# Local attention: where the softmax weights are divided by their sums, and which way round the values are multiplied

## The chip, the cores and the metric

The kernel runs on one core of a Trainium2 chip. A core has five engines, each with its own queue of instructions that it works off in the order written: PE (TensorE, matrix products into PSUM), DVE (VectorE), ACT (ScalarE), POOL (GpSimd) and SP (SyncE, which here issues transfers). They run side by side and wait for one another through semaphores. The metric is the time of one execution on the device in microseconds; lower is better.

## The reference

The program is one forward pass through four stages, each added to its input: six layers of an attention with a distance term, a mixture of experts, a state-space block, and a local transformer of two layers. Only the last stage is touched. Its attention works on B = 8 sequences of 256 tokens, with 8 heads of 64 features. Cut to what matters:

```python
q = l2norm(q) * qs;  k = l2norm(k) * ksc
q, k = rotary_xpos(q, k)
# windows of 64 queries; each sees its own 64 keys and the 64 before
sim  = einsum('bhwid,bhwjd->bhwij', bq * 8, bk)
sim  = where(mask, -max, sim)                 # i < j or i > j + 64 or j == -1
attn = softmax(sim, axis=-1)
out  = einsum('bhwij,bhwjd->bhwid', attn, bv)
x    = x + out_as_rows @ wo                   # then a gated feed-forward
```

The softmax may be divided by its sum before or after the product with the values. The result is the same up to rounding.

## The kernel before, in words

Local attention is `attention(l, b, t0)`: one block is one layer l (2) and one sequence b (8), 16 blocks in all. A block handles its 256 tokens as two chunks c of 128 queries. Chunk 0 takes keys 0 to 127. Chunk 1 is two windows of 64 queries: queries 128 to 191 with keys 64 to 191, and queries 192 to 255 with keys 128 to 255. So values are needed from three starting points: `("v", 0)`, `("v", 1)` and `("v", 2)` begin at token 0, 64 and 128. `P` is 128 and `HF` is 64.

The steps of a block are these, with the lines of the kernel before.

- `project` (1284): queries, keys or values from the tokens, one 128x512 bank of PSUM each. There are 7 projections: two chunks of keys and of queries, three of values. `value` (1290) copies the values to SBUF on ACT.
- `square` and `norms` (1295, 1315): squares on ACT and their sums over a head on DVE. `inverse` (1320 to 1322) makes the inverse norms: a maximum on DVE, then a logarithm and an exponential on ACT.
- `rotate` (1303 to 1307): three multiplies on DVE into r1 and r2 (three buffers each); `add` (1326) on POOL sums them; `unit_keys` (1330) on POOL scales the keys, a 128x512 tile by a column for each head.
- `turn` and `turned` (1338, 1344): transposes on PE, and the copy to SBUF on ACT.
- `scores` (1351, 1360): the mask is added by a matmul with the identity, then the products; `top` (1371, 1374): the negated maximum of each row on DVE.
- `expo(c, par)` (1383): exponentials on ACT of four of the eight heads (par 0 the even ones, par 1 the odd ones); each also leaves its row sum in `rz`.
- `turn_e` and `turned_e` (1392, 1399, 1401): the exponentials are transposed, four heads at a time; the copy is DVE's for even heads, ACT's for odd ones.
- `values` (1409): the turned exponentials are the weights of the matmul, the values stream through; the output has tokens on the partitions.
- `divide` (1416, 1418): reciprocal of the sums and a multiply on DVE, from PSUM into o.
- `turn_o` and `turned_o` (1426, 1432): o is transposed, so that features are on the partitions, and copied to `ot` on ACT.
- `out_proj` (1437) and `residual` (1443): the product with wo, and the addition to the tokens on DVE.

Around these stand `enter` (1256 to 1271), which normalises and turns the next sequence in the first layer, and `feed_forward` (1471 to 1540), once for each two sequences: turn_in, stats, scale (its `rs`, lines 81 and 82 on POOL), norm (hk, line 1242), products pg and pa (1500), gelu (1506, with loads of an activation table on both sides), pff (1520), and a residual `y<-pff` (1532).

The order of the work is written out by hand. Every step is put down with `at(slot, order, fn)`. A block begins 16 slots after the one before it, so up to three pieces of different blocks are interleaved. The slots are then worked through in order, inside a slot by the number `order`, and with equal numbers by who was put down first. What a step issues goes to the end of the queue of each engine it uses. No scheduler changes this order. PSUM has 8 banks here: 3 for scores, and 5 that all other products share; a product waits until one of these is free.

```python
(13, 4, turn_e, 0, 0), (13, 4, turn_e, 0, 1), (14, 4, turned_e, 0, 0), (14, 2, turned_e, 0, 1),
(15, 4, values, 0, 0), (15, 4, values, 0, 1), (17, 2, divide, 0), (18, 2, turn_o, 0), (19, 3, turned_o, 0),
```

Of the kernel before, what the change touches and what calls it, by code (L numbers as in the profile page):

```python
# [10 lines left out]
F32 = mybir.dt.float32  # L11
# [3 lines left out]
ALU = mybir.AluOpType  # L15
# [3 lines left out]
P = 128  # L19
# [16 lines left out]
DEPTH1, HEADS1, DH1, WIN = 2, 8, 64, 64  # L36
# [19 lines left out]
def model_kernel(ctx: ExitStack, tc: tile.TileContext, A: dict, out: bass.AP):  # L56
    nc = tc.nc
# [3 lines left out]
    small = ctx.enter_context(tc.tile_pool(name="small", bufs=4))  # L61
# [10 lines left out]
    ident = const.tile([P, P], F32, name="ident", tag="ident")  # L72
# [108 lines left out]
    with ExitStack() as s0:  # L181
# [3 lines left out]
        wk = s0.enter_context(tc.tile_pool(name="wk", bufs=2))  # L185
# [4 lines left out]
        ps_m = s0.enter_context(tc.tile_pool(name="ps_m", bufs=2, space=PSUM))  # L190
# [11 lines left out]
        for b in range(NB):  # L202
            h = hp.tile([P, NC, P], F32, name="h", tag=f"h{b}")
# [24 lines left out]
        def at(slot, order, fn):  # L228
            slots.setdefault(slot, []).append((order, len(slots[slot]) if slot in slots else 0, fn))
# [645 lines left out]
    with ExitStack() as s2:  # L875
        c2 = s2.enter_context(tc.tile_pool(name="c2", bufs=1))
        wk = s2.enter_context(tc.tile_pool(name="swk", bufs=2))
# [3 lines left out]
        ps_m = s2.enter_context(tc.tile_pool(name="ps_mm", bufs=1, space=PSUM))  # L881
# [301 lines left out]
    with ExitStack() as s3:  # L1183
        c3 = s3.enter_context(tc.tile_pool(name="c3", bufs=1))
        wk = s3.enter_context(tc.tile_pool(name="lwk", bufs=2))
        ps_s = s3.enter_context(tc.tile_pool(name="ps_sl", bufs=3, space=PSUM))
        ps_m = s3.enter_context(tc.tile_pool(name="ps_ml", bufs=5, space=PSUM))
# [6 lines left out]
        HF = P // 2  # L1194
# [81 lines left out]
        def attention(l, b, t0):  # L1276
            v = {}
# [8 lines left out]
                v["p", key] = pq  # L1286

            def value(key):
                vt = wk.tile([P, INNER], F32, name="v", tag=f"v{key}")
                nc.scalar.copy(vt, v["p", key])  # L1290
                v["v", key] = vt

            def square(c, i):
# [83 lines left out]
            def expo(c, par):  # L1377
                if par == 0:
                    v["e", c] = wk.tile([P, 2, 4, P], F32, name="el", tag="el")
                    v["rz", c] = small.tile([P, HEADS1], F32, name="rz", tag="rz", bufs=3)  # L1380
                for j in range(4):
                    h = 2 * j + par
                    nc.scalar.activation(  # L1383
                        v["e", c][:, par, j, :], v["s", c][par][:, j, :], AF.Exp,
                        scale=v["rn", c][:, 0, h : h + 1], bias=v["nm", c][:, par, j : j + 1],
                        accum_out=v["rz", c][:, h : h + 1],
                    )

            def turn_e(c, par):
                pt = ps_m.tile([P, 4, P], F32, name="pte", tag="m")  # L1390
                for j in range(4):
                    nc.tensor.transpose(pt[:, j, :], v["e", c][:, par, j, :], ident)  # L1392
                v["pe", c, par] = pt
# [6 lines left out]
                else:  # L1400
                    nc.scalar.copy(v["et", c][:, par], v["pe", c, par])

            def values(c, half):
                if half == 0:
                    v["pav", c] = ps_m.tile([P, HEADS1, DH1], F32, name="pav", tag="m")
                for h in range(4 * half, 4 * half + 4):
                    hd = h * DH1
                    for q0, nq, key in [(0, P, 0)] if c == 0 else [(0, HF, 1), (HF, HF, 2)]:
                        nc.tensor.matmul(  # L1409
                            v["pav", c][q0 : q0 + nq, h, :], v["et", c][:, h % 2, h // 2, q0 : q0 + nq],  # L1410
                            v["v", key][:, hd : hd + DH1], start=True, stop=True,
                        )

            def divide(c):
                rz = v["rz", c]
                nc.vector.reciprocal(rz, rz)
                o = wk.tile([P, HEADS1, DH1], F32, name="o", tag="o")
                nc.vector.tensor_tensor(  # L1418
                    o, v["pav", c], rz.unsqueeze(2).to_broadcast([P, HEADS1, DH1]), ALU.mult
                )  # L1420
                v["o", c] = o.rearrange("p h d -> p (h d)")

            def turn_o(c):
                pt = ps_m.tile([P, 4, P], F32, name="pto", tag="m")
                for k in range(4):
                    nc.tensor.transpose(pt[:, k, :], v["o", c][:, k * P : (k + 1) * P], ident)
                v["po", c] = pt

            def turned_o(c):
                if c == 0:  # L1430
                    v["ot"] = wk.tile([P, 4, T], F32, name="ot", tag="ot")
                nc.scalar.copy(v["ot"][:, :, c * P : (c + 1) * P], v["po", c])

            def out_proj():
                pn = ps_m.tile([P, T], F32, name="pn", tag="m")
# [9 lines left out]
            for slot, order, fn, *args in (  # L1445
                (0, 3, project, (0, 1), 1, 0), (1, 4, square, 0, 1), (1, 4, rotate, 0, 1), (2, 5, norms, 0, 1), (2, 6, add, 0, 1),
                (1, 3, project, (0, 0), 0, 0), (2, 4, square, 0, 0), (2, 4, rotate, 0, 0), (3, 5, norms, 0, 0), (3, 6, add, 0, 0),
                (4, 5, inverse, 0), (5, 6, unit_keys, 0),
                (2, 3, project, 0, 2, 0), (3, 4, value, 0),
                (3, 3, project, (1, 1), 1, P), (4, 4, square, 1, 1), (4, 4, rotate, 1, 1), (5, 5, norms, 1, 1), (5, 5, add, 1, 1),  # L1450
                (4, 3, project, (1, 0), 0, P), (5, 4, square, 1, 0), (5, 4, rotate, 1, 0), (6, 5, norms, 1, 0), (6, 6, add, 1, 0),
                (7, 5, inverse, 1), (8, 6, unit_keys, 1),
                (5, 3, project, 1, 2, HF), (6, 4, value, 1),
                (6, 3, project, 2, 2, P), (7, 4, value, 2),
                (5, 5, turn, 0, 0), (6, 5, turned, 0, 0), (7, 5, turn, 0, 1), (8, 3, turned, 0, 1),
                (8, 5, turn, 1, 0), (9, 4, turned, 1, 0), (10, 4, turn, 1, 1), (11, 4, turned, 1, 1),
                (9, 3, scores, 0), (10, 2, top, 0), (11, 3, expo, 0, 0), (12, 3, expo, 0, 1),
                (12, 3, scores, 1), (13, 2, top, 1), (14, 3, expo, 1, 0), (15, 3, expo, 1, 1),
                (13, 4, turn_e, 0, 0), (13, 4, turn_e, 0, 1), (14, 4, turned_e, 0, 0), (14, 2, turned_e, 0, 1),
                (15, 4, values, 0, 0), (15, 4, values, 0, 1), (17, 2, divide, 0), (18, 2, turn_o, 0), (19, 3, turned_o, 0),  # L1460
                (16, 4, turn_e, 1, 0), (16, 4, turn_e, 1, 1), (17, 3, turned_e, 1, 0), (17, 3, turned_e, 1, 1),
                (18, 4, values, 1, 0), (19, 4, values, 1, 1), (20, 2, divide, 1), (21, 2, turn_o, 1), (22, 3, turned_o, 1),
                (23, 4, out_proj), (24, 3, residual),
            ):
                at(t0 + slot, order, lambda fn=fn, args=args: fn(*args))

# [84 lines left out]
        for n in range(DEPTH1 * NB):  # L1551
            l, b = n // NB, n % NB
            if l == 0:
                enter(b, SLOTS * n)
            attention(l, b, SLOTS * n)
            if b % 2 == 1:
                feed_forward(l, b - 1, SLOTS * n)
# [96 lines left out]
```

## Time and profile before

| what | value |
|---|---|
| three runs | 2004.97, 2005.86, 2011.44 us; median 2005.86 us |
| profiled execution | 2002.59 us, its span 2000.8 us |
| mean granted clock of PE | 0.944 |
| PE busy | 1702.5 us (85%) |
| DVE busy | 1441.5 us (72%) |
| ACT busy | 1285.3 us (64%) |
| POOL busy | 1107.4 us (55%) |
| local transformer, first to last | about 1520 us to 2000.8 us of the span |

Durations in what follows are of the profiled execution. A busy PE is not PE at its peak, as matmuls overlap and their ends are modelled. A line number is one of the kernel before, if not said otherwise. In an answer in order of time the columns are start, length, engine and line; a bracket says how long the engine stood idle before it and what released it.

### The profile page before, as it was taken

To read this page: it belongs to the slowest core of one execution; us is meant where nothing else is said; L and a number is where in the kernel's file an instruction comes from. 1 tells how busy PE (TensorE), PEld (TensorE's weight loads), DVE (VectorE), ACT (ScalarE), POOL (GpSimd) and SP (SyncE) were. 2 spreads that over 40 slices of the span, in tenths; PEclk is the share of its full clock that TensorE was granted. 3 is DMA by queue.
4 is the path that set the end of the run, shared out by engine and by line. 5 is a ranking of instruction groups with operands and counts; after the bars stand their busy time and mean duration, and the time that the engine had idled before them with its cause. 6 is when DMAs were issued, how large, how long until landed. Compare 5 with 4: busy or idle time off the path is not lost. (4 is left out here: it accounts for less than half of the span.)

```text
span 2000.8 us, 38671 instructions
## 1 busy us (share of the span) xinstructions
PE 1702.5 (85%) x13390; PEld 999.1 (50%) x13406; DVE 1441.5 (72%) x3339; ACT 1285.3 (64%) x4570; POOL 1107.4 (55%) x1641
## 2 busy tenths in 40 slices
PE   5899999999999999998768867687666898888987
PEld 2565655655655655655444542222122555555554
DVE  4778787878787878786655436988897777666664
ACT  4787888888888888886541324443532666666664
POOL 2477777777777777777763024767564332233221
PEclk9999999999999999998888979888878999999999
DMA  9200000000000000000000310000000000000000
GB/s 306 70 2 2 21 4 2 15 11 1 8 17 2 2 24 2 2 2 4 7 5 7 111 38 2 4 6 0 1 0 1 1 1 1 1 1 1 6 6 11
DMA packets 43218, 35.52 MB, mean 18 GB/s; under 512 B 3957, under 2 KB 39055, under 8 KB 43023
## 3 DMA queue, kind: packets, MB, share of 16 engines
q1 hardware_dynamic: 41423, 30.63, 5.0%
q8 instruction: 108, 1.77, 0.4%
q0 software_dynamic: 1024, 2.10, 0.4%
q14 instruction: 87, 0.71, 0.1%
q10 hardware_dynamic: 576, 0.31, 0.1%
HBM read 20.57 MB, written 12.45 MB: 17 GB/s over the span
## 5 line engine op out<-in xcount | busy, mean ns | idle before, releaser
L334 ACT ACTIVATE e<-s,nmax 128x256 f32<-128x256 f32 x1536 | 708.9, 490 | 96.2 <-DVE nmax L330 93.2
L330 DVE TENSOR_REDUCE nmax<-s 128x2 f32<-128x512 f32 x768 | 493.9, 671 | 147.0 <-PE s L320 146.9
L334 ACT ACTIVATION_READ_ACCUMULATOR e<-s,nmax 128x1 f32 x1536 | 341.4, 222 | 0.0
L320 PE MATMUL s<-kt,qm 32*128 32x256 f32 x3072 | 304.9, 423 | 18.4 <-ACT e L334 15.8
L371 PE MATMUL pacc<-e,dg 128*32 128x256 f32 x3072 | 257.5, 396 | 41.7 <-POOL dg L344 28.5
L320 PEld LDWEIGHTS s<-kt,qm 32*128 32x128 f32 x3072 | 184.5, 191 | 116.2 <-ACT e L334 65.9
L1104 POOL TENSOR_TENSOR hc<-h,bc 128x1024 f32<-128x1024 f32 x64 | 155.4, 2433 | 114.3 <-DVE h L1097 106.1
L1326 POOL TENSOR_TENSOR r<-r,r 128x512 f32<-128x512 f32 x64 | 81.1, 1271 | 225.5 <-DVE r L1307 179.5
L344 POOL TENSOR_TENSOR dg<-sel,z 128x256 f32<-128x256 f32 x192 | 118.4, 617 | 132.2 <-DVE z L342 113.4
L1086 ACT ACTIVATE da<-pd,na 128x510 f32<-128x510 f32 x128 | 80.8, 682 | 166.2 <-PE pd L1069 154.5
L371 PEld LDWEIGHTS pacc<-e,dg 128*32 128x32 f32 x3072 | 95.8, 111 | 166.1 <-POOL dg L344 61.1
L1097 DVE TENSOR_TENSOR_SCAN h<-da,pu 128x1024 f32<-128x1024 f32 x64 | 146.4, 2287 | 8.5 <-DVE pu L1095 0.5
L81 POOL TENSOR_SCALAR rs<-mv 128x2 f32<-128x2 f32 (+1 forms) x192 | 44.3, 230 | 190.3 <-DVE mv L237 103.4
L82 POOL TENSOR_TENSOR rs<-rs,mhalf 128x2 f32<-128x2 f32 (+1 forms) x192 | 140.4, 732 | 15.7
L1383 ACT ACTIVATE el<-sl,nm,rn 128x128 f32<-128x128 f32 x256 | 114.0, 466 | 37.7 <-DVE nm L1374 37.5
L1069 PE MATMUL pu<-u,ssel 32*128 32x512 f32 x256 | 95.0, 749 | 49.8 <-DVE h L1097 39.9
L1283 PE MATMUL pq<-wqkv,y 128*128 128x512 f32 x224 | 119.7, 620 | 1.0 <-DVE y L1271 1.0
L381 ACT ACTIVATE nw<-pacc 128x256 f32<-128x256 f32 x96 | 36.9, 384 | 118.6 <-PE pacc L367 117.6
L459 PE MATMUL pf<-h2t,wa 128*128 128x256 f32 x384 | 106.9, 402 | 0.0
L475 PE MATMUL po<-wf,r 128*128 128x128 f32 x768 | 101.9, 288 | 2.4 <-DVE r L469 2.4
L475 PEld LDWEIGHTS po<-wf,r 128*128 128x128 f32 x768 | 93.6, 198 | 16.9 <-DVE st L235 13.6
L302 POOL TENSOR_TENSOR qm<-qt,kmask 128x1024 f32<-128x1024 f32 x48 | 90.9, 1895 | 0.4 <-DVE qt L291 0.4
(302 smaller groups left out, 3480.9 us busy)
## 6 DMA issues: line engine op xcount, KB each, us to landing
bucket<-zrow SPq DMA_DIRECT2D x1, 8640.0 KB
ln<-in_ln_dram SPq DMA_DIRECT2D x6, 448.0 KB, 3.7
wa<-in_wa_dram SPq DMA_DIRECT2D x6, 384.0 KB, 3.1
wf<-in_wf_dram SPq DMA_DIRECT2D x6, 256.0 KB, 2.7
wqkv<-in_wqkv_dram SPq DMA_DIRECT2D x1, 1536.0 KB, 6.2
xb<-bucket SPq DMA_DIRECT2D x23, 64.0 KB, 1.9
routed<-ob SPq DMA_DIRECT2D x23, 64.0 KB, 1.6
w<-in_w1e_dram SPq DMA_DIRECT2D x1, 1408.0 KB, 33.4
```

What stands on the lines that cost most here:

```text
L82: nc.gpsimd.tensor_tensor(dst, dst, mhalf.to_broadcast(list(dst.shape)), ALU.pow)
L320: nc.tensor.matmul(ss[g][:, i, :], v["qm"][rows, 2 * k + i].rearrange("p j q -> p (j q)"), v["kt"][rows, :], start=True, stop=True,)
L330: nc.vector.tensor_reduce(v["nmax", k][:, g, :], v["s", k][g], AX.X, ALU.max, negate=True)
L334: nc.scalar.activation(v["e", k][:, g, i, :], v["s", k][g][:, i, :], AF.Exp, bias=v["nmax", k][:, g, i : i + 1], accum_out=v["z", k][:, g, ...
L344: nc.gpsimd.tensor_tensor(dg, sel32.unsqueeze(1).to_broadcast(sh), z.unsqueeze(2).to_broadcast(sh), ALU.mult)
L371: nc.tensor.matmul(acc, v["dg", k][:, 2 * g + i, :], v["e", k][:, g, i, :], start=(g == 0), stop=False,)
L459: nc.tensor.matmul(pf[:, i, :], v["w"][0][:, f0 : f0 + P], v["h2t"], start=True, stop=True)
L475: nc.tensor.matmul(po[:, c, :], v["r"][:, f, c * P : (c + 1) * P], v["w"][1][:, f, :], start=(f == 0), stop=(f == 3),)
L1097: nc.vector.tensor_tensor_scan(h.rearrange("p h t -> p (h t)"), da, pu.rearrange("p h t -> p (h t)"), 0.0, ALU.mult, ALU.add)
L1104: nc.gpsimd.tensor_tensor(hc, v["h", n], v["bc", 1].unsqueeze(1).to_broadcast([P, 2, T2]), ALU.mult)
L1283: nc.tensor.matmul(pq, yb[:, col : col + P], wqkv[:, l, i * INNER : (i + 1) * INNER], start=True, stop=True)
L1383: nc.scalar.activation(v["e", c][:, par, j, :], v["s", c][par][:, j, :], AF.Exp, scale=v["rn", c][:, 0, h : h + 1], bias=v["nm", c][:, par ...
```

## The change

Three things are changed in a block of local attention.

1. The exponentials are divided by their sums before they are turned. `divide(c, par)` now takes four heads: a reciprocal on DVE, and a multiply of 128x512 on POOL, in place.
2. In `values` weights and streamed operand swap places. The values of one head (128x64) are the weights and the turned, divided exponentials stream through. The output has features on the partitions, two heads to a bank half each, which is what `out_proj` wants. So `turn_o` and `turned_o` are gone; `valued` copies the product to `ot`, on ACT for chunk 0 and on DVE for chunk 1.
3. The values from token 64 on are not projected; POOL copies them from the second half of `("v", 0)` and the first half of `("v", 2)`.

The list of steps is written anew to suit. out_proj stands at slot 21 (before 23), residual at slot 22 (before 24).

```diff
             def value(key):
                 vt = wk.tile([P, INNER], F32, name="v", tag=f"v{key}")
-                nc.scalar.copy(vt, v["p", key])
+                if key == 1:
+                    nc.gpsimd.tensor_copy(vt[0:HF, :], v["v", 0][HF:P, :])
+                    nc.gpsimd.tensor_copy(vt[HF:P, :], v["v", 2][0:HF, :])
+                else:
+                    nc.scalar.copy(vt, v["p", key])
...
+            def divide(c, par):
+                rz = v["rz", c][:, par, :]
+                nc.vector.reciprocal(rz, rz)
+                e = v["e", c][:, par]
+                nc.gpsimd.tensor_tensor(e, e, rz.unsqueeze(2).to_broadcast([P, 4, P]), ALU.mult)
...
+            def values(c):
+                v["pav", c] = ps_m.tile([P, 4, P], F32, name="pav", tag="m")
+                for j in range(4):
                     for q0, nq, key in [(0, P, 0)] if c == 0 else [(0, HF, 1), (HF, HF, 2)]:
-                        nc.tensor.matmul(
-                            v["pav", c][q0 : q0 + nq, h, :], v["et", c][:, h % 2, h // 2, q0 : q0 + nq],
-                            v["v", key][:, hd : hd + DH1], start=True, stop=True,
-                        )
-            def divide(c):
-                rz = v["rz", c]
-                nc.vector.reciprocal(rz, rz)
-                o = wk.tile([P, HEADS1, DH1], F32, name="o", tag="o")
-                nc.vector.tensor_tensor(
-                    o, v["pav", c], rz.unsqueeze(2).to_broadcast([P, HEADS1, DH1]), ALU.mult
-                )
-            def turn_o(c):
...
-            def turned_o(c):
+                        for par in range(2):
+                            hd = (2 * j + par) * DH1
+                            nc.tensor.matmul(
+                                v["pav", c][HF * par : HF * par + HF, j, q0 : q0 + nq],
+                                v["v", key][:, hd : hd + DH1], v["et", c][:, par, j, q0 : q0 + nq],
+                                start=True, stop=True,
+                            )
+            def valued(c):
                 if c == 0:
                     v["ot"] = wk.tile([P, 4, T], F32, name="ot", tag="ot")
-                nc.scalar.copy(v["ot"][:, :, c * P : (c + 1) * P], v["po", c])
+                    nc.scalar.copy(v["ot"][:, :, 0:P], v["pav", c])
+                else:
+                    nc.vector.tensor_copy(v["ot"][:, :, P:], v["pav", c])
...
-                (5, 3, project, 1, 2, HF), (6, 4, value, 1),
-                (6, 3, project, 2, 2, P), (7, 4, value, 2),
+                (6, 3, project, 2, 2, P), (7, 4, value, 2), (8, 6, value, 1),
...
-                (13, 4, turn_e, 0, 0), (13, 4, turn_e, 0, 1), (14, 4, turned_e, 0, 0), (14, 2, turned_e, 0, 1),
-                (15, 4, values, 0, 0), (15, 4, values, 0, 1), (17, 2, divide, 0), (18, 2, turn_o, 0), (19, 3, turned_o, 0),
-                (16, 4, turn_e, 1, 0), (16, 4, turn_e, 1, 1), (17, 3, turned_e, 1, 0), (17, 3, turned_e, 1, 1),
-                (18, 4, values, 1, 0), (19, 4, values, 1, 1), (20, 2, divide, 1), (21, 2, turn_o, 1), (22, 3, turned_o, 1),
-                (23, 4, out_proj), (24, 3, residual),
+                (12, 2, divide, 0, 0), (13, 3, divide, 0, 1), (13, 4, turn_e, 0, 0), (14, 4, turn_e, 0, 1),
+                (14, 4, turned_e, 0, 0), (15, 2, turned_e, 0, 1), (16, 3, values, 0), (17, 3, valued, 0),
+                (15, 2, divide, 1, 0), (16, 3, divide, 1, 1), (16, 4, turn_e, 1, 0), (17, 4, turn_e, 1, 1),
+                (17, 3, turned_e, 1, 0), (18, 2, turned_e, 1, 1), (19, 3, values, 1), (20, 3, valued, 1),
+                (21, 4, out_proj), (22, 4, residual),
```

More of the change, by code (lines that the diff above doesn't have):

```diff
@@ L1379, in expo @@
                     v["e", c] = wk.tile([P, 2, 4, P], F32, name="el", tag="el")
-                    v["rz", c] = small.tile([P, HEADS1], F32, name="rz", tag="rz", bufs=3)
+                    v["rz", c] = small.tile([P, 2, 4], F32, name="rz", tag="rz", bufs=3)
                 for j in range(4):
@@ L1385, in expo @@
                         scale=v["rn", c][:, 0, h : h + 1], bias=v["nm", c][:, par, j : j + 1],
-                        accum_out=v["rz", c][:, h : h + 1],
+                        accum_out=v["rz", c][:, par, j : j + 1],
                     )
+            def divide(c, par):
[3 more added lines that the diff above has]
+                nc.gpsimd.tensor_tensor(e, e, rz.unsqueeze(2).to_broadcast([P, 4, P]), ALU.mult)
             def turn_e(c, par):
@@ L1401, in turned_e @@
                     nc.scalar.copy(v["et", c][:, par], v["pe", c, par])
[L1403 to L1407, printed above, removed]
-                    for q0, nq, key in [(0, P, 0)] if c == 0 else [(0, HF, 1), (HF, HF, 2)]:
-                        nc.tensor.matmul(
-                            v["pav", c][q0 : q0 + nq, h, :], v["et", c][:, h % 2, h // 2, q0 : q0 + nq],
-                            v["v", key][:, hd : hd + DH1], start=True, stop=True,
-                        )
@@ L1414, in divide @@
-            def divide(c):
-                rz = v["rz", c]
-                nc.vector.reciprocal(rz, rz)
-                o = wk.tile([P, HEADS1, DH1], F32, name="o", tag="o")
-                nc.vector.tensor_tensor(
-                    o, v["pav", c], rz.unsqueeze(2).to_broadcast([P, HEADS1, DH1]), ALU.mult
-                )
-                v["o", c] = o.rearrange("p h d -> p (h d)")
-            def turn_o(c):
[L1424 to L1427, printed above, removed]
```

## The prediction

> **What bounds the kernel now.** I read the page first (busy shares, slices), then busy time by stretch, the chain that ended last in order of time, and the instructions of one block in order of time. The edits touch only local attention, from 1529 us (first query-key-value projection, line 1283) to the end. A stretch that leaves out its start and end, columns length and busy PE, weight load, DVE, ACT, POOL, then clock, DMA share and rate:
>
> ```profile
> 1590.00:1975.00 385.00, 339.11 (x2433) 216.16 (x2445) 262.45 (x626) 251.78 (x739) 112.73 (x118) 0.97 0.01 3
> ```
>
> PE is busy 88%, DVE 68%, ACT 65%, POOL 29%. PE looks like the bound; the chain says otherwise. One block, from its first score matmul to the next block's (start, length, what):
>
> ```profile
> 1734.96 1.21 PE sl L1360 x16
> 1736.18 1.28 DVE nm L1371 x2
> 1737.74 1.87 ACT el L1383 x8
> 1740.14 1.10 PE sl L1360 x32
> 1741.24 1.02 PE pte L1392 x8
> 1742.49 2.58 PE pff L1520 x6
> 1745.07 1.73 PE pav L1409 x16
> ...
> 1752.35 1.19 DVE rn L1315 x2
> 1758.36 1.20 DVE rn L1315 x2
> 1761.00 1.21 PE sl L1360 x16
> ```
>
> The chain passes between PE, DVE and ACT; no engine carries it alone. From one score start S to the next I read three kinds of block in this chain: 2 plain ones (24.6, 25.2 us), 7 in which a gelu runs (29.15 to 30.16, mean 29.8), 6 in which a feed-forward's last product pff runs (26.0 to 26.7, mean 26.3), then a last block with the tail. In the block above, the DVE, in order of time:
>
> ```profile
> 1745.10 1.98 DVE L1532 SCALAR_TENSOR_TENSOR y<-pff,b2c,y 64x256 f32<-64x256 f32 x4 [1.19 <-PE pff L1520]
> 1749.74 0.69 DVE L1303 TENSOR_TENSOR r<-pq,tab 128x512 f32<-128x512 f32 x1 [0.86 <-ACT sq L1295]
> 1757.00 0.69 DVE L1303 TENSOR_TENSOR r<-pq,tab 128x512 f32<-128x512 f32 x1 [1.22 <-ACT sq L1295]
> 1759.58 0.25 DVE L1320 TENSOR_SCALAR rn<-rn 128x16 f32<-128x16 f32 x1
> 1762.19 0.69 DVE L1371 TENSOR_REDUCE nm<-sl 128x4 f32<-128x512 f32 x1 [1.61 <-PE sl L1360]
> ```
>
> From 1745.1 to 1760.6 it idles only 2.1 us: it sets the next scores as much as PE does. The last rotation (1757.00) is followed by norms, inverse norm (1759.58), logarithm and exponential on ACT and the copy of turned keys; then come the scores.
>
> **What the skill says.** "TensorE: Matmul & The Clock Gate", section "Architectural detail", calls DVE and ACT strict first-in first-out; the trace agrees (the rotation idles 1.22 us with other work behind it). "TensorEngine Tiling (Array Packing)", "When to Use Tiling", advises swapping stationary and streaming operands when the free dimension is at most 64. The trace agrees: 16 records of pav with 128x64 weights take 0.69 us, with 128x128 weights 2.0. "GPSIMD Engine Reference", 3.1, gives 769 ns for a tight loop over 512 elements; no POOL copy is in this trace. "SBUF — State Buffer", "Who interferes with whom", describes a port pair that DVE and GpSimd lock; POOL's multiply at line 1330 stays at 1040 to 1052 ns in all 32 cases, so no lock shows here.
>
> **The change part by part, busy time.** The rows (window 1590 to 2001, 14 blocks of pav and pto):
>
> ```profile
> L1283 PE MATMUL pq<-wqkv,y 128*128 128x512 f32 x182 | 97.0, 614 | 0.0
> L1330 POOL TENSOR_TENSOR r<-r,rn 128x512 f32<-128x512 f32 x27 | 28.2, 1044 | 31.8 <-ACT rn L1322 26.9 <-DVE y L1443 4.9
> L1409 PE MATMUL pav<-v,et 128*128 128x64 f32 x224 | 28.4, 282 | 2.2 <-DVE et L1399 2.2
> L1426 PE MATMUL pto<-ident,o 128*128 128x128 f32 x112 | 17.1, 276 | 4.3 <-DVE o L1418 4.3
> ```
>
> PE, each block: the middle-value projection goes, 97.0/91 = 1.07 us; eight pto transposes go, 17.1/14 = 1.22; the values of chunk 0 cost 28.4/14 = 2.03 and become 16 records with 64-column weights and 128 streamed columns. That form isn't in the trace: at least 16 x 43 ns = 0.69 (the 64x64 form), at most 2.03; I take 1.16 (the 64x128 score records, 16.3/14), a saving of 0.87. Sum 3.16 us, 50.6 over 16 blocks. ACT: one value copy (0.60) and two copies of pto (1.17) go, one copy of pav (0.58) comes: -1.2. DVE: two multiplies by the reciprocals (1.38) and two reciprocals (0.39) go; four reciprocals (at most 0.19 each) and one copy (0.69) come: -0.3. POOL: four multiplies of line 1330's form, 4 x 1.04 = 4.2, and two 64x512 copies, an estimate of 0.77 each from the page named (bounds 0.64 and 1.27, half and all of the two-operand row at line 1326): +5.7. The copies stand behind unit_keys, which ends at S+0.65, and POOL's next work is at S+3.4 or later, so they are hidden up to 1.4 us each; beyond that they would delay what follows one for one. POOL at 14 of 30 us is no bound by load. No DMA moves.
>
> **What is moved, and the waits.** I follow the new order by hand through the pff block above, times from S. Exponentials of (0,0) end at 4.54; reciprocal 4.60 to 4.80; POOL's divide 4.85 to 5.89. Behind it on POOL stands the feed-forward's rs (lines 81, 82: 1.0 us), which now ends at 6.97, before at 5.08:
>
> ```profile
> 1739.02 0.22 POOL L81 TENSOR_SCALAR rs<-mv 128x2 f32<-128x2 f32 x1 [3.40 <-DVE mv L1232]
> 1739.32 0.72 POOL L82 TENSOR_TENSOR rs<-rs,mhalf 128x2 f32<-128x2 f32 x1
> 1751.24 2.53 POOL L1326 TENSOR_TENSOR r<-r,r 128x512 f32<-128x512 f32 x2 [11.20 <-DVE r L1307]
> ```
>
> hk waits for rs (to 7.73), and top(1) is queued behind hk on DVE: 7.65 to 9.22, before 6.34 to 7.90. So (1,0)'s exponentials run 9.3 to 11.1. The reciprocal of (0,1) comes after top(1); its divide ends at 10.5, pff (delayed with hk's transpose) at 10.75, turn_e(0,1) at 11.35, its ACT copy at 12.0. That copy now stands ahead of (1,1)'s exponentials, which end at 13.7, before 11.54. The reciprocal of (1,1) waits for them, and on DVE y<-pff (1.98) is queued behind it: it starts at 13.95 instead of 10.14.
>
> From there DVE runs without a gap: y<-pff 1.98, et 0.69, two rotations 2.72, norms 1.27, valued(1) 0.69, so valued(1) ends near 21.3. out_proj (1.99) waits for it, and turn(0,0) (0.6) now stands behind out_proj: 23.9. The fourth rotation needs that transpose (its r1 has three buffers): 23.9, before 22.04. Then rotation 1.36, norm 0.64, the residual 0.85, which now precedes the last norm, norm 0.64, inverse 0.25, ACT 0.2 + 0.3, copy 0.59: next scores at 28.7, before 26.05. Against the six blocks' mean of 26.3 that is +2.4.
>
> Gelu block: the same delays up to (1,1)'s exponentials (13.6). On ACT the second square (0,0) is queued behind et(1,1), whose transpose stands behind a pg on PE: it ends at 17.8, before 14.95. The second rotation follows to 19.2, norms to 20.4, valued(1) to 21.1, out_proj to 23.4, which now stands before the last value projection and the last pg. Value copy to 25.5 (26.3 if its PSUM bank comes from the copy of turn(0,0)), table load 1.28, gelus 1.83, table load 1.28, logarithm to copy 1.1: scores at 31.0 to 31.8. I take 31.4: +1.6.
>
> Plain blocks lack pff, y<-pff and gelu: exponentials of (1,1) to 12.2, second square behind et(1,1), second rotation to 17.1, valued(1) 19.1, turn(0,0) 21.7, scores 26.6: +2 on 24.6. The last block's out_proj starts at 18.6 instead of 17.3 (its yo takes the place of y<-pff): +1.3.
>
> Sum: 7 x 1.6 + 6 x 2.4 + 2 x 2 + 1.3 = 31; taken as **+30**, since ends are rounded up. The profiled execution took 2002.59 us (span 2000.8 and 1.8 around it): 2032.6. The median of three runs, 2005.86, lies 3.3 above it, so I forecast 2036.
>
> Unknown costs: pav(0) at 2.03 instead of 1.16 lies on the gelu path only (7 x 0.9 = +6), at 0.69 it gains 3; POOL's multiply at 1.27 (line 1326's price) is passed twice in each block: +7; it cannot be cheaper than a one-operand 0.77: -8. Half a microsecond of error at the end of each walk is +-8.
>
> **Rivals.** *PE decides, faster.* For it: 88% busy, and from 1746.6 to 1759 no PE gap above half a microsecond. Then the 3.16 us removed pay, less some 0.9 for the ACT copy that now stands alone between turn_e(0,1) and the values: 16 x 2.2 = 36, 1970. Its place is the stretch after the values of chunk 0; it decides if the later start of y<-pff and the rotations stays under what PE saves, 3.2 us. I find 3.8 in pff blocks, so the margin is small there. Against: DVE idles only 2.1 us in that stretch and saves 0.3.
>
> *The delays half cancel.* The wait of rs or of the fourth rotation falls in slack that I don't see: +-12 around 2006, more above than below.
>
> *POOL dearer.* The multiply at double the row, from lock or overhead: two passes a block, 15 x 2.1 = 31 more: 2067. Against: line 1330 has the same shape and broadcast and no spread.
>
> That the change doesn't do what it says can't be: the removed projections and transposes are absent from the new order.
>
> **Chances.** Queue order, slower, own range 2018 to 2054: 0.68. PE decides: 0.13. Half cancelled: 0.14 (0.03 faster, 0.06 within, 0.05 slower). POOL dearer: 0.05. A difference under 0.3% (6 us) can't be told from no change. Faster 0.16, same 0.06, slower 0.78. The range, 2000 to 2058, leaves out the second and fourth case (0.18) and cuts the low end of the third.
>
> **What would show it.** Right: rs of the feed-forward ends near S+7; top(1) near S+9.2; y<-pff starts over 3 us later; the fourth rotation waits for PE's turn(0,0); score starts 28 to 29 and 31 to 32 us apart; PE's share of the stretch falls to some 72% ((339 - 43)/(385 + 26)). Wrong: score starts under 26 and 29.8 us apart, with DVE idle ahead of PE; or a divide far from 1.04 us; or pav(0) near 2 us.

## The result and the profile after

The changed kernel takes 2055.4 us (median of four runs, 2050.8 to 2061.1) against 2005.8 us before on the same chip: a ratio of 1.0242, 95% interval 1.0210 to 1.0274. It is slower by about 50 us; the forecast was +30. The profiled execution took 2056.27 us, span 2054.5.

In the lines below, line numbers from 1283 on are those of the changed kernel, about 5 higher than in the kernel before (score matmuls are L1365, the multiply of `divide` is L1398, `values` is L1421). First the busy times of the stretch of blocks, columns as in the prediction (length; busy PE, weight load, DVE, ACT, POOL; granted clock, DMA share, rate):

```profile
1590.00:2025.00 435.00, 347.93 (x2296) 208.51 (x2310) 258.43 (x646) 242.94 (x714) 191.19 (x205) 0.89 0.01 2
```

PE's share is 80%. It does less work than before and runs it at a clock of 0.89 where the stretch of before had 0.97. Up to the first scores the two kernels differ by 1.3 us only (1543.92 against 1542.64).

From one score start to the next, in us:

| blocks | before | forecast | after | difference to before |
|---|---|---|---|---|
| first plain, second plain | 24.6, 25.2 | 26.6 (+2 on each) | 27.6, 30.0 | +2.9, +4.9 |
| 7 with a gelu, mean | 29.8 | 31.4 | 33.6 | +3.8 each |
| 6 with pff, mean | 26.3 | 28.7 | 29.2 | +2.8 each |
| last, to the end of the span | 41.7 | +1.3 | 42.8 | +1.1 |

The sum is 2.9 + 4.9 + 7 x 3.8 + 6 x 2.8 + 1.1 + 1.3 (before the first scores) = 54, which is the difference of the two spans (53.7). So the loss lies in these blocks but for the 1.3 us. In a pff block of after, the chain of work in order of time (start, length, what), from its first scores to the next:

```profile
1760.39 1.21 PE sl L1365 x16
1761.61 1.28 DVE nm L1376 x2
1763.19 1.88 ACT el L1388 x8
1765.10 0.19 DVE rz L1396
1765.42 1.04 POOL el L1398
1766.73 0.73 POOL rs L82
1767.49 0.42 DVE hk L1242
1768.60 2.58 PE pff L1519 x6
...
1781.29 1.99 PE pn L1437 x8
1783.29 0.45 PE ptq L1343 x4
1788.60 1.21 PE sl L1365 x16
```

The chain now passes through POOL: the reciprocal, the multiply, then the feed-forward's rs behind it, and only then hk and pff. It also passes through out_proj (pn). Neither POOL's multiply nor out_proj stood in the chain of this block before. The DVE in the same block:

```profile
1767.49 0.73 DVE L1242 TENSOR_SCALAR hk<-ptn,mv,rs 128x128 f32<-128x128 f32 x2 [1.58 <-POOL rs L82]
1768.13 1.28 DVE L1376 TENSOR_REDUCE nm<-sl 128x4 f32<-128x512 f32 x2
1774.05 0.18 DVE L1396 RECIPROCAL rz<-rz 128x4 f32<-128x4 f32 x1 [2.23 <-ACT el L1388]
1774.14 1.95 DVE L1531 SCALAR_TENSOR_TENSOR y<-pff,b2c,y 64x256 f32<-64x256 f32 x4
1783.86 0.69 DVE L1308 TENSOR_TENSOR r<-pq,tab 128x512 f32<-128x512 f32 x1 [1.28 <-PE ptq L1343]
```

With S = 1760.39 these are the steps of the forecast's walk: rs ends at S+7.1 (forecast 7.0), top(1) at S+9.0 (9.2; the two reductions of line 1376 overlap hk), y<-pff starts at S+13.75 (13.95), the fourth rotation at S+23.5 (23.9) and waits for PE's turned tile, the next scores start at S+28.2 (28.7). This block is the shortest of the six; the others take 28.9 to 29.95 us. Of the wait for the turned tile only some 0.1 us is its own: the last square on ACT, for which this rotation waited before the change, ends at 1783.65, and the turned tile at 1783.72. The operations that the trace of before could only bound (line, engine, shapes and count; busy us, mean ns; idle time before and what ended it):

```profile
L1398 POOL TENSOR_TENSOR el<-el,rz 128x512 f32<-128x512 f32 x56 | 58.4, 1042 | 103.5 <-DVE rz L1396 103.5
L1421 PE MATMUL pav<-et,v 128*64 128x128 f32 x224 | 28.5, 352 | 3.1 <-ACT et L1412 2.8
L1292 POOL COPY v<-v 64x512 f32<-64x512 f32 x14 | 8.5, 607 | 0.9
```

The multiply costs 1.042 us (1.04 taken), a POOL copy 0.61 (0.77 estimated), and no engine waited for the copies. The values of chunk 0 cost 28.5/14 = 2.04 us a block on average, as much as before (2.03), where 1.16 was taken. The next view shows why. One gelu block, one of the three that take 34.6 us (the other four take 32.7 to 33.0), from its first scores in steps of 5 us:

```profile
1912.54:1917.54 5.00, 3.78 (x23) 3.17 (x24) 2.08 (x7) 1.75 (x7) 1.86 (x3) 0.66 0.00 0
1917.54:1922.54 5.00, 3.46 (x39) 1.94 (x38) 2.17 (x6) 2.79 (x13) 1.95 (x3) 0.69 0.02 3
1922.54:1927.54 5.00, 3.59 (x20) 2.57 (x20) 1.49 (x6) 4.23 (x17) 2.08 (x2) 0.50 0.00 0
1927.54:1932.54 5.00, 5.00 (x16) 2.63 (x16) 2.02 (x5) 1.36 (x3) 1.28 (x2) 0.79 0.00 0
1932.54:1937.54 5.00, 5.00 (x44) 2.84 (x43) 4.06 (x9) 1.98 (x4) 2.29 (x2) 1.00 0.00 0
```

The clock (third number from the end) is 0.5 to 0.8 in the first four of these steps and 1.0 in the fifth. PE in order of time in the same block:

```profile
1912.54 2.05 PE L1365 MATMUL sl<-qkt 64*128 64x128 f32 x16 [0.81 <-ACT qkt L1349]
1918.14 0.38 PE L1356 MATMUL sl<-maskb,identb 128*128 128x512 bf16 x1 [1.81 <-ACT el L1388]
1919.80 1.11 PE L1403 MATMUL pte<-ident,el 128*128 128x128 f32 x4
1923.89 1.11 PE L1403 MATMUL pte<-ident,el 128*128 128x128 f32 x4 [2.12 <-POOL el L1398]
1924.94 2.71 PE L1421 MATMUL pav<-et,v 128*64 128x128 f32 x16
1927.58 2.08 PE L1283 MATMUL pq<-wqkv,y 128*128 128x512 f32 x2
1931.72 0.60 PE L1403 MATMUL pte<-ident,el 128*128 128x128 f32 x4
```

Four transposes of one form take 1.11 us here and 0.60 eight microseconds later. The 16 score records at the start of the block are at half pace already (2.05 us; 1.16 at full pace), after waits of 1.1 us at most in the seven microseconds before. In all seven gelu blocks the values of chunk 0 run wholly or mostly at half pace; in the pff blocks they do not. The wait of 1.81 us ahead of the mask of chunk 1 has its like before the change (2.52 us in a gelu block there). The wait of 2.12 us for POOL's multiply is new, and after it the values (2.71 us) and a projection (2.08) run at half pace; that this wait is the cause is tested below. "TensorE: Matmul & The Clock Gate" of the Trainium skill, in "A second HAM failure mode: psum-queue depth-cycling", describes the like in another kernel, where PE's short idle pieces came from cycling through the banks of PSUM: it idles often enough that its clock swings between half and full. The trace agrees that short pieces are enough (the waits here are for ACT and POOL). The same page's rule, in "HAM oscillation — how this bites in real kernels", puts the limit at gaps of 3.4 us; here the longest gap from the first scores on is 2.7 us, and the clock is at half all the same, so the measurement decides.

### The profile page after: what moved, and what is told of

Same layout as the page of the kernel before. It is cut to its first block, busy times and chain, and to the rows that moved or that the text cites. A ratio compares the mean times of both kernels' runs of the same rounds, so it can differ in the third digit from the quotient of the medians.

```text
span 2054.5 us, 38364 instructions
## 1 busy us (share of the span) xinstructions
PE 1708.9 (83%) x13230; PEld 988.8 (48%) x13246; DVE 1434.7 (70%) x3355; ACT 1272.4 (62%) x4538; POOL 1193.2 (58%) x1737
## 5 line engine op out<-in xcount | busy, mean ns | idle before, releaser
L1398 POOL TENSOR_TENSOR el<-el,rz 128x512 f32<-128x512 f32 x64 | 66.7, 1043 | 113.9 <-DVE rz L1396 113.9
L1283 PE MATMUL pq<-wqkv,y 128*128 128x512 f32 x192 | 107.1, 658 | 6.0 <-ACT qkt L1349 4.7
```

The source lines that it names most:

```text
L1283: nc.tensor.matmul(pq, yb[:, col : col + P], wqkv[:, l, i * INNER : (i + 1) * INNER], start=True, stop=True)
```

## The experiments

Two theories were tested. *Queue order*, the forecast: new waits in in-order queues delay what stands behind them, in three places (rs behind the multiply on POOL; y<-pff behind the reciprocal on DVE; turn, last value projection and residual behind an earlier out_proj). *Clock*, formed from the profile after: a part of the loss is PE at half pace after its new waits. The rival from the prediction was *PE decides*: what PE no longer does pays. Where a run is set against the changed kernel, this is done by the two ratios to the kernel before, as the runs are from several chips. Such a difference of two ratios is itself uncertain by 0.002 to 0.0045, 5 to 9 us.

**The rs of the feed-forward ahead of the multiply.** One number in the list of steps puts `divide(0,0)` later in its slot.

```diff
-                (12, 2, divide, 0, 0), ...
+                (12, 5.5, divide, 0, 0), ...
```

> The changed kernel with the first divide (0,0) put behind the feed-forward's rs in its slot. Queue-order theory: rs ends near S+5.1 again, top(1) starts 1.3 us earlier, the exponentials of (1,1) end 1.0 to 1.4 us earlier in 14 blocks, and that reaches the next scores: 14 to 20 us faster than the changed kernel, 2036 to 2042 us. Rival, the delay of rs falls in slack (the first divide then ends 1.2 us later and takes its place): within 4 us of 2055.

Measured 2040.2 us, ratio 1.0189 (1.0166 to 1.0212): 0.0053 to 0.0068 below the changed kernel, 11 to 14 us. POOL in a pff block of this run (S = 1754.65):

```profile
1758.78 0.22 POOL L81 TENSOR_SCALAR rs<-mv 128x2 f32<-128x2 f32 x1 [2.16 <-DVE mv L1232]
1759.08 0.72 POOL L82 TENSOR_TENSOR rs<-rs,mhalf 128x2 f32<-128x2 f32 x1
1759.78 1.04 POOL L1398 TENSOR_TENSOR el<-el,rz 128x512 f32<-128x512 f32 x1
```

rs ends at S+5.15 again (before the change S+5.08, after it S+7.06). The first plain block has no rs behind the multiply, and its length is 27.57 us in both kernels; the second falls from 30.0 to 27.7, the gelu blocks from 33.6 to 32.05, the pff blocks from 29.2 to 28.6. The first place is confirmed, with less than the 14 to 20 us expected. The clock rises too, from 0.89 to 0.91 between the first scores and the end.

**y<-pff ahead of the reciprocal.**

```diff
-                (15, 2, divide, 1, 0), (16, 3, divide, 1, 1), ...
+                (15, 2, divide, 1, 0), (16, 4.5, divide, 1, 1), ...
```

> The changed kernel with the divide (1,1) put behind y<-pff in its slot, so that the feed-forward's residual no longer stands on DVE behind a reciprocal that waits for the last exponentials. My prediction made this the start of the DVE chain. Theory that y<-pff sets the chain: the six pff blocks lose 2 us each, 12 us faster than the changed kernel, 2043 us. Rival, the second square behind et(1,1) on ACT then holds the second rotation (it ended at S+16.9 in the pff block of the trace, the rotation began at 17.7): at most 0.8 in each, 0 to 5 us faster, 2050 to 2055 us.

Measured 2046.0 us, ratio 1.0202 (1.0185 to 1.0219); the changed kernel, run again beside it, 1.0257. So 0.0055 less, 11 us: the expected total, but not from where it was expected. A pff block becomes 0.8 us shorter (28.4), and so 6 x 0.8 = 5 us come from there; a gelu block, in which no y<-pff stands, becomes 0.7 shorter too, another 5. DVE in a pff block of this run:

```profile
1767.24 1.95 DVE L1531 SCALAR_TENSOR_TENSOR y<-pff,b2c,y 64x256 f32<-64x256 f32 x4
1769.56 0.18 DVE L1396 RECIPROCAL rz<-rz 128x4 f32<-128x4 f32 x1 [0.37 <-ACT el L1388]
1770.43 0.69 DVE L1410 COPY et<-pte 128x512 f32<-128x512 f32 x1 [0.69 <-PE pte L1403]
1772.84 0.69 DVE L1308 TENSOR_TENSOR r<-pq,tab 128x512 f32<-128x512 f32 x1 [0.46 <-ACT sq L1300]
1778.66 0.69 DVE L1308 TENSOR_TENSOR r<-pq,tab 128x512 f32<-128x512 f32 x1 [1.35 <-POOL r L1331]
```

y<-pff is out of the way, but three waits take its place: for the transpose, for the second square on ACT (which stands behind the copy et(1,1)), and for POOL's sum of an earlier rotation. That is what the rival expected for pff blocks. The block shown is not shorter at all (28.56 us; 28.2 for the one at the same place in the changed kernel): the mean falls through the others, of which three took some 29.3. What these and the gelu blocks gained was not isolated. All seven gelu blocks take 32.9 us here, so the long kind (34.6) is gone; the clock of the stretch from the first scores to the end rose from 0.89 to 0.90.

**out_proj and residual at their old slots.**

```diff
-                (21, 4, out_proj), (22, 4, residual),
+                (23, 4, out_proj), (24, 4, residual),
```

> The changed kernel with out_proj and residual back in their old slots (23 and 24), so that turn(0,0), the last value projection and the last pg stand before out_proj. Queue-order theory: gelu blocks gain about 1.9 us (7 of them), the others 1.0 (a residual of 0.85 off the path of the last norm): about 20 us faster than the changed kernel, 2030 to 2040 us. Rival, the second square or DVE load sets the rotations anyway: under 6 us.

Measured 2027.4 us, ratio 1.0132 (1.0108 to 1.0156): 0.0110 to 0.0125 less, 22 to 25 us, the largest of the three. Gelu blocks fall to 31.35 us, pff blocks to 27.6, plain ones to 26.6 and 27.8, and the clock rises to 0.94, so that the gain of the gelu blocks is order and pace together. In a pff block the gain is not where the walk put it. The fourth rotation of such a block of this run, in the DVE's order of time (in the changed kernel it waited 1.28 us for PE's turned tile):

```profile
1767.79 0.69 DVE L1308 TENSOR_TENSOR r<-pq,tab 128x512 f32<-128x512 f32 x1 [1.16 <-issue]
```

The block starts at 1744.45, so this is S+23.34, hardly earlier than S+23.47. PE's turn is long done (1765.63). The profile names no releaser, but the last square on ACT ends at 1767.70, 0.09 us before the rotation, as it did in the kernel before (0.08 us there, and named). So this square holds the rotation, or something that ends with it. The 0.9 us that this block gains is the residual (0.85) that no longer stands ahead of the last norm; the other pff blocks gain more (1.6 on average over all six), which was not isolated.

**All three moves together.** The edits are those of the three diffs above.

> The changed kernel with all three moves: rs ahead of the first divide, y<-pff ahead of the last, out_proj and residual in their old slots. Queue-order theory: the gains of the two already measured add (15 and 28 us at the median), with a little for the third: 2008 to 2018 us. Rival, they overlap because the same rotations wait: 2020 to 2027 us.

Measured 2016.8 us, ratio 1.0047 (1.0033 to 1.0062): 0.0210 less than the changed kernel beside it, 42 us. The single moves add up to 12.5 + 11 + 23.5 = 47, so within their uncertainty they do not overlap. pff blocks are back at 26.5 us (26.3 before the change), and the fourth rotation there starts at S+21.5. Four fifths of the loss is the order of the list, not the operations; what the order does to PE's pace is part of that (the clock is 0.91 here). What is left, some 10 us, lies in gelu blocks (30.9 against 29.8) and the two plain ones (26.6 and 27.7 against 24.6 and 25.2).

**The copied middle values alone.** The kernel before, with part 3 of the change only.

```diff
-                nc.scalar.copy(vt, v["p", key])
+                if key == 1:
+                    nc.gpsimd.tensor_copy(vt[0:HF, :], v["v", 0][HF:P, :])
+                    nc.gpsimd.tensor_copy(vt[HF:P, :], v["v", 2][0:HF, :])
+                else:
+                    nc.scalar.copy(vt, v["p", key])
...
-                (5, 3, project, 1, 2, HF), (6, 4, value, 1),
-                (6, 3, project, 2, 2, P), (7, 4, value, 2),
+                (6, 3, project, 2, 2, P), (7, 4, value, 2), (8, 6, value, 1),
```

> The kernel before with the third part alone: no middle projection, its values copied by POOL. Theory that DVE and the queues set the pace: PE loses 1.07 us of work in each block, but the next scores move little, 0 to 8 us faster than before (1998 to 2006 us). Rival, PE decides: 16 x 1.07 = 17 us faster, 1989 us. POOL's two copies take 0.61 us each and stay hidden.

Measured 1999.25 us, ratio 0.9983 (0.9970 to 0.9997). The stretch of before's prediction view, in this run:

```profile
1590.00:1975.00 385.00, 327.45 (x2408) 212.14 (x2420) 261.04 (x623) 245.57 (x725) 128.22 (x145) 0.98 0.01 3
```

PE is busy 327 us where it was 339, with no new wait in the order, and the kernel gains 3 to 4 us of the 17 that this projection took on PE (16 x 1.07). So *PE decides* falls: the interval allows 0.6 to 6 us, not 17.

**The changed kernel once more.** Control for the second set of runs.

> The changed kernel itself, on the chip of the three runs sent with it, so that they have their own base: 2050 to 2061 us, 1.021 to 1.027 of before. Both theories expect the same.

Measured 2057.8 us, ratio 1.0257 (1.0240 to 1.0274). Its blocks have the same mean lengths (33.6 and 29.2) and the same clock (0.89).

**PE kept awake, in all blocks.** The changed kernel with needless mask matmuls in PE's waits: six ahead of the scores of chunk 1 and four ahead of the second transposes. What they write is overwritten by the matmul that follows, so nothing of the computation is changed.

```diff
+                for _ in range(6 if c == 1 else 0):
+                    nc.tensor.matmul(
+                        ss[0].rearrange("p j t -> p (j t)"), identb, maskb[:, c].rearrange("p j t -> p (j t)"),
+                        start=True, stop=True,
+                    )
...
+                    for _ in range(4 if (c, par) == (0, 1) else 0):
+                        nc.tensor.matmul(
+                            pt.rearrange("p j t -> p (j t)"), identb, maskb[:, c].rearrange("p j t -> p (j t)"),
+                            start=True, stop=True,
+                        )
```

> The changed kernel with needless matmuls in PE's two waits of each block: six masks into the score bank before chunk 1's mask, four into the bank of the second transpose of chunk 0; both are overwritten. Clock theory (the 20 us that the prediction lacks come from a lower granted clock after PE's longer waits): the clock of the stretch rises from 0.89 to over 0.95, the values of chunk 0 in gelu blocks fall from 2.7 to about 1.2 us, 10 to 18 us faster than the changed kernel, 2037 to 2045 us. Rival, the clock is a bystander and the queues alone set the time: no gain, 2052 to 2062 us.

Measured 2045.3 us, ratio 1.0222 (1.0191 to 1.0254), only 4 to 7 us less, which the intervals do not tell from nothing and which lies between what the two sides expected. What was bought and paid shows in the blocks. PE in a gelu block:

```profile
1719.55 0.38 PE L1361 MATMUL sl<-maskb,identb 128*128 128x512 bf16 x1 [1.24 <-ACT el L1393]
1720.02 1.10 PE L1370 MATMUL sl<-qkt 64*64 64x128 f32 x32
1725.24 0.66 PE L1413 MATMUL pte<-ident,el 128*128 128x128 f32 x4 [1.41 <-POOL el L1403]
1726.58 1.09 PE L1431 MATMUL pav<-et,v 128*64 128x128 f32 x14 [0.31 <-ACT et L1422]
1727.59 1.12 PE L1283 MATMUL pq<-wqkv,y 128*128 128x512 f32 x2
```

The same two waits, with the fills in them and so shorter, and full pace after them: 0.66 us for the transposes, 1.5 for the values (two more records stand ahead of these 14), 1.12 for the projection. Gelu blocks fall to 31.6 us, close to the forecast's 31.4. The plain ones fall to 26.0 and 27.3. But the pff blocks become 0.9 us longer (30.1), as their PE had no time to spare there, and the last block 5 us. It happened to run at half pace from 2012 us on in this run (out_proj 3.78 us instead of 1.99).

**PE kept awake, pff blocks left out.** The same fills, only where the block's number is even or the block is the second plain one.

```diff
-                for _ in range(6 if c == 1 else 0):
+                for _ in range(6 if c == 1 and (b % 2 == 0 or (l, b) == (0, 1)) else 0):
...
-                    for _ in range(4 if (c, par) == (0, 1) else 0):
+                    for _ in range(4 if (c, par) == (0, 1) and (b % 2 == 0 or (l, b) == (0, 1)) else 0):
```

> The changed kernel with the needless matmuls (six and four) only in the blocks without pff. Clock theory: gelu blocks near 31.5 us instead of 33.6, plain ones near 26.5, pff blocks as in the changed kernel (29.2) or less; about 16 us faster than the changed kernel, 2036 to 2042 us. Rival, the gain of filled gelu blocks is paid back in the pff blocks that follow them: pff blocks at 30 again, under 8 us faster.

Measured 2038.8 us, ratio 1.0171 (1.0151 to 1.0191): 0.0086 below the changed kernel beside it, 17 us. pff blocks stay at 29.1, gelu blocks are at 32.05 (four at 31.3, three at 33.0, so the pace is not held in all of them), the plain ones at 26.0 and 27.3. The clock is 0.96. With the order left as it is and the pace mostly held, most of what came on top of the forecast goes: the clock theory holds.

**The same for the kernel before.** Six fills a block (none in the second plain one), ahead of the scores of chunk 1 or, in pff blocks and the last, of chunk 0.

```diff
+                for _ in range(6 if (c == 1 and b % 2 == 0) or (c == 0 and b % 2 == 1 and (l, b) != (0, 1)) else 0):
+                    nc.tensor.matmul(
+                        ss[0].rearrange("p j t -> p (j t)"), identb, maskb[:, c].rearrange("p j t -> p (j t)"),
+                        start=True, stop=True,
+                    )
```

> The kernel before with six needless masks into the score bank ahead of chunk 1's scores in even blocks and ahead of chunk 0's scores in odd ones (after the gelu). Clock theory: before, the stretch already runs at 0.97, so little is to be gained: 0 to 5 us faster than before. Rival, the fills gain by themselves in any kernel, as in the changed one: 10 us or more.

The stretch of the prediction's first view, in this run:

```profile
1590.00:1975.00 385.00, 350.88 (x2540) 217.83 (x2538) 262.69 (x631) 253.88 (x740) 111.66 (x118) 1.00 0.01 3
```

Measured 1996.5 us, ratio 0.9966 (0.9954 to 0.9979), 7 to 9 us less, between what the two sides expected. Gelu blocks fall from 29.8 to 29.16 us, nearly all alike; pff blocks stay at 26.3. So the kernel before lost something to the clock as well, though less than half of what the changed one lost.

**The copied middle values with the same fills.** The kernel of the copied middle values alone, with the lines of the last diff added.

> The third part alone in the kernel before, with the same fills. Theory: gelu blocks all fall to the faster of the two lengths seen in the third part alone (28.65 instead of a mean of 29.56), 7 x 0.9 = 6 us on top of its 4: 1993 to 1998 us where before has 2004. Rival, the fills do nothing: 1999 to 2001 us.

Measured 1994.97 us, ratio 0.9951 (0.9934 to 0.9968). Gelu blocks take 28.67 us but for one (30.34). This is the fastest of all kernels here, about 10 us below the kernel before; from the one without the copies it can't be told apart for sure, as the two intervals overlap.

**All three moves with the same fills.** The changed kernel with the three moved entries and the lines of the last diff.

> All three moves of order in the changed kernel, with the same fills. Theory: what is left of the loss (12 us) is the clock, 0.91 in this stretch: gelu blocks at 29 to 30 us instead of 30.9, 1998 to 2008 us. Rival, the longer way from exponentials to values costs it: 2013 us or more.

The same stretch in this run:

```profile
1590.00:1975.00 385.00, 328.00 (x2404) 196.23 (x2403) 255.97 (x644) 240.11 (x718) 190.33 (x204) 0.98 0.01 3
```

Measured 2001.96 us, ratio 0.9986 (0.9977 to 0.9994). Gelu blocks take 29.15 us and pff blocks 26.31, as in the filled kernel before (29.16 and 26.33); the plain ones stay at 26.6 and 27.7, 4.4 us more than before. Set against the filled kernel before, the full change costs 0.0020, 4 us. PE is busy 23 us less in this stretch than in that kernel's, some 1.6 us a block (the forecast took 3.16 off), and on average a block is not shorter by it. The average hides two kinds. Four gelu blocks take 28.6 us and four pff blocks 25.4 or 26.0, 0.5 to 0.7 less than in the filled kernel before. Three gelu blocks (29.5 to 30.2) and one pff block (28.73) are longer, and in each of these PE runs in part at half pace. In the pff block two rs stand on POOL ahead of the moved multiply, PE waits 1.03 us for it, and then:

```profile
1689.41 3.60 PE L1524 MATMUL pff<-g,wg 128*128 128x512 f32 x6
```

At full pace these six records take 2.74 us. So where the pace holds, the change is worth half a microsecond a block or a little more, and loses it again in these four blocks and the two plain ones. Order and pace overlap little: the three moves are worth 42 us without fills and 37 with them, the fills 17 us in the changed order and 12 in the mended one (not quite the same fills).

## Why the prediction was right in its sign and too small

- **The bound.** Right. PE's 88% was not what decided: 17 us off PE without new waits gave 3 to 4 us, and the whole change with the order and the clock mended gave 0.5 to 0.7 us in the better blocks and nothing on average.
- **The three queue places.** Right that they decide: 42 of the 50 us go when they are undone. The first (rs) was worth 11 to 14 us. The second (y<-pff) was overrated as a step: in pff blocks 0.8 us where its own delay was 3.6 (13.75 against 10.14), since the second square and POOL's sum stood ready to hold the chain; the run's other 5 us, in gelu blocks, are not accounted for. The third (out_proj) was right as a place, but in pff blocks through the residual ahead of the last norm and not through turn(0,0): the fourth rotation starts at S+23.3 without that wait too. The walk left out the last square on ACT, which ends just before the rotation in both runs.
- **The walk of a pff block.** In the block shown above, right to half a microsecond at the steps set beside it, and in its end: 28.2. Over all six blocks it is 28.2 to 29.95, mean 29.2, for 28.7.
- **The walk of a gelu block.** This is the step that failed in size: +1.6 forecast, +3.8 measured, 7 x 2.2 = 15 of the 24 us that the profiled difference (53.7) has over the forecast's 30. The second plain block gives 3 more, pff blocks 3, the time before the first scores 1.3. The walk took PE's durations at full pace: 1.16 for the values of chunk 0 (at full pace 1.5 in two pieces; at half pace up to 2.71), 0.6 for four transposes (1.11), 1.07 for a projection (2.08). With the pace held, gelu blocks take 31.6 us in one run and 32.05 in the other (31.3 where it holds, 33.0 where it does not), for the forecast's 31.4. That the kernel as a whole then takes 2038.8, for 2036, is in part luck, as the pff blocks are longer than forecast and the first plain one shorter.
- **What it was compared with.** The same walk was set against a mean (29.8) that already held half-pace stretches; held at full pace, the kernel before takes 29.16. So 0.66 of each gelu block's missing 2.2 us is this: a full-pace sum compared with a mixed-pace mean. Over seven blocks that is some 5 us. In time, fills gain 17 us after and 7 us before; the difference, some 10 us, is an estimate of the cost of clock that the change itself brings. It is rough, as the fills differ and three gelu blocks lose pace in spite of them. How the rest of the missing 20 us divides, the runs do not settle.
- **Bounds of the unknown costs.** The range gave 2.03 us for the values as a cost that could add 6 us. It came true on average (2.04), and not for the reason considered: the records are no dearer, the clock was lower. The other cost in that range, a multiply at 1.27, did not come. The measured 2055 us lies just above the 2018 to 2054 given to the queue order itself and inside the whole range to 2058. Of the two costs that were reckoned to add to it, one came by another way and one not at all, so that the result still falls inside is in part luck. At full pace the swap of weights and streamed operand, which "TensorEngine Tiling (Array Packing)", "When to Use Tiling", advises by the free dimension, does pay: all 16 records take 1.5 us in two pieces (1.09 for 14 of them), against 1.9 to 2.0 for 16 of the old form. The prediction's 16 records at 0.69 us did not show this yet, as they make half the output.
- **POOL.** Right: 1.042 us a multiply, copies hidden. *POOL dearer* falls, and DVE is not held up by it either (y<-pff 1.95 us after, 1.98 before; a rotation's first multiply 0.69 in both). The copy at 0.61 is below the 769 ns that "GPSIMD Engine Reference", 3.1, gives for 512 elements and that the estimate took.
- **What was to be seen.** pff blocks 28 to 29 us apart (28.2 to 29.95), rs at S+7, top(1) at S+9, y<-pff over 3 us later, the fourth rotation waiting for PE: all seen, the last for only 0.1 us of its own. Gelu blocks 31 to 32 apart: 32.7 to 34.6. PE's share near 72%: it was 80%, because PE took longer for less work. That a lower clock hides itself as a busy PE should have been said there.

## What to carry to other kernels

Work taken off the busiest engine is worth only what the chain of waits gives back; here 17 us of it gave 4. Before a step goes to another engine's in-order queue, list the small instructions behind it there (here a 1 us rs) and who waits for them: moving three entries of a list, with the same instructions, gave 42 us. Price a new wait on PE with its clock too: reckon PE's durations at both paces for what follows the wait, compare like with like, and try needless matmuls in the gap, but not where PE is the next to be late.

## What the runs showed of the hardware

- PE falls to half pace without a long gap: in the changed kernel no wait from the first scores on is above 2.7 us, and its clock there is 0.89. After waits of 1.8 and 2.1 us, some 6 us apart, it is 0.50 over 5 us (four transposes 1.11 us instead of 0.60).
- The length of one wait does not tell the pace after it: after the same wait of 2.5 us the 32 score records take 1.10 us in some blocks and 1.98 or 1.99 in others, in the kernel before and in the changed one. In the recorded clock of both, each stretch at one pace among these blocks lasts 3.413 us or a whole multiple of it.
- Six needless matmuls a block (1.46 us of PE time at that place) made an already tuned kernel 7 us faster, ratio 0.9966 (0.9954 to 0.9979).
- A POOL copy of 64x512 from one half of the partitions to the other takes 0.61 us, a multiply of 128x512 by a column for each head 1.04 us, with a spread of 1039 to 1087 ns over all 64 of them.
